# Adaptive-norm block with a long convolution and a Strassen FFN: the second layer norm moved from the convolution phase into the FFN's first pass

## Chip, cores, metric

One core of a Trainium2 chip. The metric is the device time of one execution in microseconds (us).

## What is computed

Input `u` is [4, 1024, 2048]: 4 batches of 1024 rows. A conditioning vector per batch gives six modulation vectors of 2048 (`sa, ca, ga` for the convolution, `sb, cb, gb` for the FFN). Cut to what matters:

```python
mod = (_silu(c) @ wmod).reshape(4, 6, 1, -1)
sa, ca, ga, sb, cb, gb = (mod[:, i] for i in range(6))
ga, gb = clip_magnitude(ga, 0.25), clip_magnitude(gb, 0.25)
h = _layernorm(x) * (1 + ca) + sa
x = x + ga * (causal_conv(h, K) + D * h)      # K: 2048 taps from the state-space parameters
h = _layernorm(x) * (1 + cb) + sb
x = x + gb * (h @ (W + low_rank).T + bias)    # 2048 x 2048
```

The convolution runs along the last axis, of 2048, so it is a multiplication of each row by a 2048 x 2048 Toeplitz matrix.

## The kernel before

The 4096 rows are 32 row tiles of 128 rows (`r`); two row tiles make one FFN unit (`u`, 16 of them). A phase for setup comes first, which computes the taps, builds the Toeplitz blocks and loads the first sections of `wmod`.

**Convolution phase, loop `r` in `net` (L925).** For each row tile:

- `conv_load` brings x (1 MB) into one of four x tiles. `stats` and `normalize` (L514, VectorE) give normalized rows in tile `n`. `conv_prep` transposes them in four groups of four 128x128 blocks (L535, TensorE against the identity, fp32, into a PSUM tile `tp`), modulates them out of PSUM with `ca`, `sa` per partition (L538, ScalarE) and splits them into fp16 high and low parts (L546, L547).
- `conv_mm` does the Toeplitz product (L567) in three families of fp16 matmuls; VectorE combines, gates and adds x (L584 to L594), which gives x1 in tile `y`, with row sums.
- `conv_post` stores x1 to DRAM (`x1d`), computes the second layer norm's mean and variance (L611, ScalarE's square with a running sum L614, `rstd`), normalizes (L617, VectorE, 128x2048, into a second `n` tile), then transposes the rows in four groups (L623, TensorE), copies each group out of PSUM (L624, ScalarE) and stores it to DRAM as `n2d` (L625, 256 KB per store).

The order is written by hand: `conv_mm` calls `tick()` ten times per row tile, and each call takes the letters of one entry of `PLAN`: S takes a step of the background work, P a step of the previous tile's `conv_post`, N one of the next tile's `conv_prep`, T the statistics and F the first step of the tile after. The background work is the merging of the low-rank update into the FFN weights (`merge`, eight parts) and the remaining modulation sections (`modps`, L317). From this order a scheduler with its own model of costs makes the final order of each engine's queue. Every engine then runs its queue in order. All large transfers are issued from SP's queue.

**FFN phase.** The FFN is a one-level Strassen product: per unit seven products of left factors (combinations of the four quarters of the transposed h, split in fp16 high and low) with seven merged weight combinations. A product is 24 matmuls of 128x512 (L704) into the PSUM tiles fX, fY, fZ. The loop has two passes `q` over the output columns. In pass 0, `left` (L645) makes the left factors of unit u+1, in program order after the matmuls of unit u: it loads `n2d` (L652, eight loads of 256 KB), modulates 16 blocks in SBUF with `cb`, `sb` (L654, ScalarE, 128x256), forms the combinations on VectorE (L671), casts them (L664, ScalarE) and takes the low part (L665, VectorE); `put` also stores each factor to `lfd` (512 KB). In pass 1, `left_again` loads the factors from `lfd`. `ffn_unit` (L693) loads the residual x1 (`xo`, two tiles of 512 KB per unit), adds the gated bias (L720), runs the products in the order 0, 4, 5, 1, 6, 2, 3, copies intermediate sums out of PSUM (L712, ScalarE: p1, p5, p6, p7), combines and gates them (`finish`, L725, L726), and stores the output once per row tile (L751, two stores of 512 KB). Unit 0's factors are made ahead, in the convolution phase.

```python
PLAN = ("PNS", "N", "NS", "NT", "PS", "PS", "PS", "PS", "FS", "SS")
...
            k.ffn_unit(pr, u, q, lf.pop(u), wc)
            if u + 1 < NU:
                lf[u + 1] = (k.left if q == 0 else k.left_again)(pr, u + 1)
```

PSUM has two tiles for transposes (`tps`), five for accumulation (`acc`) and one for modulation.

Of the kernel before, what the change touches and what calls it, by code (L numbers as in the profile page):

```python
# [24 lines left out]
P = 128  # L25
# [9 lines left out]
class Net:  # L35
# [254 lines left out]
    def prep_mod(self, pool):  # L290
# [8 lines left out]
        self.sct = self.const("sct", [P, 16, 8, NB])  # L299
# [24 lines left out]
    def mod_column(self, pool, name, plus_one):  # L324
# [7 lines left out]
        col = self.const(name, [P, NC, NB])  # L332
# [274 lines left out]
    def conv_post(self, pl, r, y, sums):  # L607
        nc, v = self.nc, self.nc.vector
        STQ(nc).dma_start(out=self.x1d[r], in_=y)
        mn = pl["sm"].tile([P, 1], F32, tag="mn", name="mn")  # L610
        v.tensor_scalar(mn, sums[:, 0:1], sums[:, 1:2], -1.0 / D, ADD, MUL)  # L611
        n = pl["n"].tile([P, D], F32, tag="n", name="n2")
        sq = pl["sm"].tile([P, 1], F32, tag="sq", name="sq")
        nc.scalar.activation(n, y, AF.Square, bias=mn, accum_out=sq)  # L614
        rs = pl["sm"].tile([P, 1], F32, tag="rs2", name="rs2")
        self.rstd(pl["sm"], sq, rs, 1, "r2", 1.0 / D)
        v.tensor_scalar(n, y, mn, rs, ADD, MUL)  # L617
        yield
        for c0 in range(0, NC, 4):
            nt = pl["nt"].tile([P, 4, P], F32, tag="nt", name="nt")  # L620
            tp = self.tps.tile([P, 4, P], F32, tag="t", name="tp2")
            for k in range(4):
                nc.tensor.transpose(tp[:, k], n[:, ds(P * (c0 + k), P)], self.ident)  # L623
            nc.scalar.copy(nt, tp)  # L624
            NTQ(nc).dma_start(out=self.n2d[r // 2][:, c0 : c0 + 4, r % 2, :], in_=nt)  # L625
            yield
# [18 lines left out]
    def left(self, pl, u):  # L645
        nc, v = self.nc, self.nc.vector
        b = u // 4
        t = pl["t"].tile([P, NC, 2, P], F32, tag="t", name="gt")
        for q in range(4):
            for h in range(2):  # L650
                sl = slice(HC * h + 2 * q, HC * h + 2 * q + 2)
                nc.sync.dma_start(out=t[:, sl], in_=self.n2d[u][:, sl])  # L652
                for c in range(sl.start, sl.stop):
                    nc.scalar.activation(  # L654
                        t[:, c], t[:, c], AF.Identity,
                        bias=self.sb[:, c, b : b + 1], scale=self.cb[:, c, b : b + 1],
                    )
        a11, a12 = t[:, 0:HC, 0, :], t[:, HC:NC, 0, :]
        a21, a22 = t[:, 0:HC, 1, :], t[:, HC:NC, 1, :]
        res = {}  # L660
# [8 lines left out]
        def comb(x, y, op, tag):  # L669
            t = pl["s"].tile([P, HC, P], F32, tag=tag, name=tag)  # L670
            v.tensor_tensor(t, x, y, op)  # L671
            return t

        put(0, a11)
        s1 = comb(a21, a22, ADD, "s1")
        put(4, s1)
        s2 = comb(s1, a11, SUB, "s2")
        put(5, s2)
        put(1, a12)
        put(6, comb(a11, a21, SUB, "s1"))  # L680
        put(2, comb(a12, s2, SUB, "s1"))
        put(3, a22)
        return res
# [9 lines left out]
    def ffn_unit(self, pl, u, q, lf, wc):  # L693
# [21 lines left out]
        xs = []  # L715
        for r in range(2):
            x = pl["o"].tile([P, 2, 512], F32, tag="o", name="xo")
            src = self.x1d[2 * u + r].rearrange("p (h n) -> p h n", h=2)[:, :, ds(512 * q, 512)]
            nc.sync.dma_start(out=x, in_=src)
            v.tensor_tensor(x, x, self.gbias, ADD)  # L720
            xs.append(x)

        def finish(r, h, cv):
            t = pl["e"].tile([P, 512], F32, tag="fin", name="fin")
            v.tensor_tensor(t, cv, self.gbt[:, h], MUL)  # L725
            v.tensor_tensor(xs[r][:, h], xs[r][:, h], t, ADD)  # L726
# [3 lines left out]
        p1 = copy("X", "p1")  # L730
        prod(4, "Y")
        p5 = copy("Y", "p5")
        prod(5, "Z")
        p6 = copy("Z", "p6")
        prod(1, "X")
        finish(0, 0, ps["X"])
        v.tensor_tensor(p6, p6, p1, ADD)
        prod(6, "Z")
# [3 lines left out]
        finish(1, 1, p7)  # L742
        prod(2, "Y")
        v.tensor_tensor(p6, p6, ps["Y"], ADD)
        finish(0, 1, p6)
        prod(3, "Z")
        v.tensor_tensor(p1, p1, ps["Z"], ADD)
        finish(1, 0, p1)
        for r in range(2):
            dst = self.io["out"][ds(256 * u + P * r, P), :].rearrange("p (h n) -> p h n", h=2)[:, :, ds(512 * q, 512)]  # L750
            STQ(nc).dma_start(out=dst, in_=xs[r])  # L751
# [7 lines left out]
PLAN = ("PNS", "N", "NS", "NT", "PS", "PS", "PS", "PS", "FS", "SS")  # L759
# [16 lines left out]
def net(ctx: ExitStack, tc: tile.TileContext, io):  # L776
# [5 lines left out]
    k.n2d = k.dram.tile([NU, P, NC, 2, P], F32, tag="n2d", name="n2d")  # L782
# [13 lines left out]
    def section(sec, pools):  # L796
# [5 lines left out]
        if sec == 0:  # L802
            k.sa = k.mod_column(msm, "sa", 0.0)
            k.hinv = k.fold_scale(msm, k.ca, k.sa, "fs1")
        elif sec == 1:
            k.ca = k.mod_column(msm, "ca", 1.0)
        elif sec == 2:
            k.gas, (k.gad,) = k.mod_gate(msm, "gad")
        elif sec == 4:
            k.cb = k.mod_column(msm, "cb", 1.0)  # L810
        elif sec == 3:
            k.sb = k.mod_column(msm, "sb", 0.0)
# [41 lines left out]
    for name, bufs in (("h", 2), ("n", 2), ("t", 2), ("y", 2), ("g", 1), ("nt", 2)):  # L854
# [33 lines left out]
    def early():  # L888
        right.close()
        for name, bufs in (("w", 1), ("l", 8), ("t", 1), ("s", 1)):  # L890
            pr[name] = pool(p2, "p2" + name, bufs, "right")
        load_w(0, ORDER[0])

# [27 lines left out]
    k.conv_late(xs.pop(0), *ys[0])  # L921
    take(k.conv_post(pl, 0, *ys[0]), 9)
    k.conv_late(xs.pop(1), *ys[1])
    post = k.conv_post(pl, 1, *ys[1])
    for r in range(2, 32):  # L925
# [6 lines left out]
        if r == LEFT0:  # L932
            while "w" not in pr:
                step()
            lf[0] = k.left(pr, 0)
# [3 lines left out]
        def tick():  # L939
            for a in next(plan):  # L940
                if a == "S":
                    step()
                elif a == "P":
# [95 lines left out]
```

## Time and profile before

| | |
|---|---|
| three runs | 2164.45 us median (2163.26 to 2166.11) |
| profiled execution | 2165.34 us, span 2163.6 us |
| granted TensorE clock, mean | 0.984 |
| TensorE busy | 2080.5 us, 11084 matmuls |
| VectorE busy | 1355.8 us |
| ScalarE busy | 938.8 us |
| DMA | 516.62 MB, mean 239 GB/s |
| last convolution matmul, first FFN matmul | 984.4 us, 984.5 us |
| start of the last FFN matmul | 2156.8 us |

In the profile PE is TensorE's matmuls, PEld its weight loads, DVE VectorE, ACT ScalarE, POOL GpSimd and SP the engine whose queue issues the DMAs. L704 is line 704 of the kernel. A group's row gives engine, operation, output and inputs, shape, count, then busy time and mean duration, then the engine's idle time in front of these instructions and what ended it. Matmuls overlap, so their busy times are longer than the distance between their starts.

### The profile page before, as it was taken

The numbers are of one execution on the slowest core, as the hardware profiler recorded it, in microseconds if no ns is written. First come the engines' busy times: TensorE is split into PE (matmuls) and PEld (weight loads), VectorE is DVE, ScalarE is ACT, GpSimd is POOL, SyncE is SP. The second block draws the span as 40 slices with busy tenths as digits, with TensorE's granted clock in tenths as the row PEclk, the third lists the DMA queues.
The fourth block names the chain that finished last, engine by engine and source line by source line (L and its number), as shares of the span: only waits on it lengthen the run. The fifth ranks groups of instructions, "written<-read, shape, count | busy, mean of one in ns | idle before, by whom it ended". The sixth has DMA issues, their size and how long they took to land.

```text
span 2163.6 us, 28506 instructions
## 1 busy us (share of the span) xinstructions
PE 2080.5 (96%) x11084; PEld 1019.0 (47%) x11084; DVE 1355.8 (63%) x2293; ACT 938.8 (43%) x1795; POOL 2.8 (0%) x12
## 2 busy tenths in 40 slices
PE   5698999999999999999999999999999999999998
PEld 1144555555555555564444444444444444444443
DVE  6538798889989999964665766666533333232333
ACT  1057677767776779862453535454200000000000
POOL 0000000000000000000000000000000000000000
PEclk8799999999999999999999999999999999999999
DMA  9988597888787657648756565656785544544541
GB/s 393 371 284 299 197 333 272 303 317 294 277 294 281 244 207 246 220 163 307 246 218 230 215 241 209 239 201 241 289 329 180 185 154 174 166 171 160 176 155 68
DMA packets 206497, 516.62 MB, mean 239 GB/s; under 512 B 15206, under 2 KB 80871, under 8 KB 179479
## 3 DMA queue, kind: packets, MB, share of 16 engines
q1 hardware_dynamic: 205824, 513.21, 66.3%
q8 instruction: 87, 1.43, 0.3%
q10 hardware_dynamic: 538, 1.59, 0.2%
q14 instruction: 48, 0.39, 0.1%
HBM read 325.89 MB, written 188.85 MB: 238 GB/s over the span
## 4 chain that ended last, share of the span: by engine, by line
PE 63%; DVE 15%; DMA 10%; ACT 9%; issue 2%; SPq 1%; POOL 0%; DVEq 0%; ACTq 0%
PE fZ L704 19%; PE fY L704 12%; PE fX L704 11%; PE ya L567 8%; PE yb L567 4%; PE modps L317 3%; DMA gt<-n2d 3%; PE lps L443 2%; ACT gt L654 2%; DVE lf L665 2%; PE tp L623 2%; ACT t L538 2%; ACT n L614 2%; DMA wm<-in_wmod 1%; DMA xo<-x1d 1%
## 5 line engine op out<-in xcount | busy, mean ns | idle before, releaser
L704 PEld LDWEIGHTS <-lf 128*128 128x128 f16 x5376 | 526.3, 98 | 643.0 <-issue 11.5
L704 PE MATMUL fZ<-w,lf 128*128 128x512 f16 x2304 | 514.8, 380 | 6.7 <-ACT p L712 6.7
L704 PE MATMUL fX<-w,lf 128*128 128x512 f16 x1536 | 342.6, 379 | 0.0
L704 PE MATMUL fY<-w,lf 128*128 128x512 f16 x1536 | 342.5, 379 | 0.0
L567 PEld LDWEIGHTS <-hc 128*128 128x128 f16 x2304 | 215.8, 98 | 190.7 <-issue 34.7
L720 DVE TENSOR_TENSOR xo<-xo,gb 128x1024 f32<-128x1024 f32 x64 | 78.4, 1224 | 207.0 <-DMA xo<-x1d 198.6
L538 ACT ACTIVATE t<-tp,sa,ca 128x128 f32<-128x128 f32 x512 | 199.6, 466 | 10.2 <-DVE sa L376 4.7
L654 ACT ACTIVATE gt<-gt,sb,cb 128x256 f32<-128x256 f32 x256 | 132.7, 592 | 151.7 <-DMA gt<-n2d 151.6
L567 PE MATMUL ya<-kh,hc 128*128 128x512 f16 (+3 forms) x768 | 192.6, 326 | 1.8 <-ACT qs L580 1.8
L567 PE MATMUL ya<-kh,hs 128*128 128x512 f16 (+3 forms) x768 | 193.3, 327 | 0.5 <-ACT hs L546 0.3
L567 PE MATMUL yb<-kh,hc 128*128 128x512 f16 (+3 forms) x768 | 193.0, 326 | 0.0
L317 PE MATMUL modps<-wm,sct 128*32 128x512 f32 x768 | 123.5, 687 | 32.2 <-DMA wm<-in_wmod 23.1
L567 PEld LDWEIGHTS <-hs 128*128 128x128 f16 x1152 | 107.6, 98 | 98.0 <-issue 17.7
L712 ACT COPY p<-fZ 128x512 f32<-128x512 f32 x64 | 37.3, 582 | 256.6 <-PE fZ L704 256.6
L712 ACT COPY p<-fX 128x512 f32<-128x512 f32 x32 | 18.5, 578 | 267.8 <-PE fX L704 254.9
L567 PE MATMUL ya<-kl,hs 128*128 128x512 f16 (+3 forms) x384 | 125.4, 326 | 0.0
L567 PE MATMUL yb<-kl,hc 128*128 128x512 f16 (+3 forms) x384 | 125.4, 326 | 0.0
L567 PE MATMUL ya<-kl,hc 128*128 128x512 f16 (+3 forms) x384 | 125.1, 326 | 0.0
L664 ACT CAST lf<-s 128x1024 f16<-128x1024 f32 x64 | 67.2, 1049 | 105.1 <-DVE s L671 78.7
L624 ACT COPY nt<-tp 128x512 f32<-128x512 f32 x128 | 74.9, 594 | 62.9 <-PE tp L623 43.3
L547 DVE TENSOR_TENSOR hc<-t,hc 128x512 f16<-128x512 f32 x128 | 87.5, 684 | 9.7 <-ACT hc L546 9.7
L535 PE MATMUL tp<-ident,n 128*128 128x128 f32 x512 | 79.4, 279 | 13.1 <-ACT t L538 11.6
(236 smaller groups left out, 2227.2 us busy)
## 6 DMA issues: line engine op xcount, KB each, us to landing
wm<-in_wmod SPq DMA_DIRECT2D x96, 1024.0 KB
lfd<-lf SPq DMA_DIRECT2D x112, 512.0 KB
lf<-lfd SPq DMA_DIRECT2D x112, 512.0 KB
x<-in_x SPq DMA_DIRECT2D x32, 1024.0 KB
x1d<-y SPq DMA_DIRECT2D x32, 1024.0 KB
n2d<-nt SPq DMA_DIRECT2D x128, 256.0 KB
gt<-n2d SPq DMA_DIRECT2D x128, 256.0 KB
xo<-x1d SPq DMA_DIRECT2D x64, 512.0 KB
```

Of the source, the lines that this page charges most:

```text
L317: self.last = self.nc.tensor.matmul(self.modps[32 * g : 32 * g + 32, :], self.sct[:, j].rearrange("p r b -> p (r b)"), w[:, ds(512 * g, 512)],
L443: nc.tensor.matmul(ps, la[:, x, k, h], y[:, k, osl], start=(n == 0), stop=(n == 5))
L535: nc.tensor.transpose(tp[:, k], n[:, ds(P * (c0 + k), P)], self.ident)
L538: nc.scalar.activation(t[:, k], tp[:, k], AF.Identity, bias=self.sa[:, c, b : b + 1], scale=self.ca[:, c, b : b + 1],)
L547: v.tensor_tensor(lo[:, sl], src, hi[:, sl], SUB)
L567: nc.tensor.matmul(pf[:, o:512], h, self.kf[f][z][:, ds(k0, 512 - o)], start=first, stop=(i == last and (x, z) == (1, 0)), skip_group_chec ...
L624: nc.scalar.copy(nt, tp)
L654: nc.scalar.activation(t[:, c], t[:, c], AF.Identity, bias=self.sb[:, c, b : b + 1], scale=self.cb[:, c, b : b + 1],)
L664: nc.scalar.copy(hl[:, :, 0, :], s)
L704: nc.tensor.matmul(ps[name], lf[i][:, k, x, :], wc[i][k // 4][:, k % 4, y, :], start=(first and n == 0), stop=(n == 3 * HC - 1), skip_grou ...
L712: nc.scalar.copy(t, ps[name])
L720: v.tensor_tensor(x, x, self.gbias, ADD)
```

## The change

`conv_post` no longer normalizes, transposes and stores `n2d`. It writes two numbers per row to a small tile `ln2`: 1/std and -mean/std. The square goes into the x tile, which has been read by then. `n` has one buffer instead of two, the `nt` and `n2d` tiles are gone.

`left` becomes a generator. Its first step loads two x1 row tiles from `x1d` (1 MB each) and normalizes each on ScalarE, in place (`x*scale + bias`, 128x2048). Eight steps follow, each with four fp32 transposes into one PSUM tile and two modulations out of PSUM (128x256) into `t`. A last step makes the seven factors, with one VectorE scratch tile and in-place operations instead of two scratch tiles. In the FFN's first pass `ffn_unit` calls `tick()` after each product, and `LPLAN` says what it takes: two transpose steps after each of the first four products, the factors after the fifth, load and normalization of the unit after next at the sixth. In the convolution phase the letter L in `PLAN` does the same for unit 0 in the last two row tiles.

`ffn_unit` also handles the residual and the output in four tiles of 256 KB per unit in place of two of 512 KB (five buffers), stores each as soon as it is done, and reuses p6, p7 and p1 for the gated values. `cb`, `sb` and the modulation inputs get their tiles from other pools.

```diff
-    def conv_post(self, pl, r, y, sums):
+    def conv_post(self, pl, r, x, y, sums):
         STQ(nc).dma_start(out=self.x1d[r], in_=y)
...
-        nc.scalar.activation(n, y, AF.Square, bias=mn, accum_out=sq)
-        rs = pl["sm"].tile([P, 1], F32, tag="rs2", name="rs2")
+        nc.scalar.activation(x, y, AF.Square, bias=mn, accum_out=sq)
+        rs = self.ln2[:, r, 1:2]
         self.rstd(pl["sm"], sq, rs, 1, "r2", 1.0 / D)
-        v.tensor_scalar(n, y, mn, rs, ADD, MUL)
-        yield
-        for c0 in range(0, NC, 4):
-            nt = pl["nt"].tile([P, 4, P], F32, tag="nt", name="nt")
-            tp = self.tps.tile([P, 4, P], F32, tag="t", name="tp2")
-            for k in range(4):
-                nc.tensor.transpose(tp[:, k], n[:, ds(P * (c0 + k), P)], self.ident)
-            nc.scalar.copy(nt, tp)
-            NTQ(nc).dma_start(out=self.n2d[r // 2][:, c0 : c0 + 4, r % 2, :], in_=nt)
-            yield
+        v.tensor_tensor(self.ln2[:, r, 0:1], mn, rs, MUL)

-    def left(self, pl, u):
+    def left(self, pl, u, res):
+        xs = []
+        for r in range(2):
+            x = pl["x2"].tile([P, D], F32, tag=f"x2{r}", name="x2")
+            nc.sync.dma_start(out=x, in_=self.x1d[2 * u + r])
+            nc.scalar.activation(
+                x, x, AF.Identity, bias=self.ln2[:, 2 * u + r, 0:1], scale=self.ln2[:, 2 * u + r, 1:2]
+            )
+            xs.append(x)
+        yield
         t = pl["t"].tile([P, NC, 2, P], F32, tag="t", name="gt")
-        for q in range(4):
-            for h in range(2):
-                sl = slice(HC * h + 2 * q, HC * h + 2 * q + 2)
-                nc.sync.dma_start(out=t[:, sl], in_=self.n2d[u][:, sl])
-                for c in range(sl.start, sl.stop):
-                    nc.scalar.activation(t[:, c], t[:, c], AF.Identity, ...)
+        for c0 in range(0, NC, 2):
+            tp = self.tps.tile([P, 2, 2, P], F32, tag="t", name="tp2")
+            for c in range(2):
+                for r in range(2):
+                    nc.tensor.transpose(tp[:, c, r], xs[r][:, ds(P * (c0 + c), P)], self.ident)
+            for c in range(2):
+                nc.scalar.activation(
+                    t[:, c0 + c], tp[:, c], AF.Identity,
+                    bias=self.sb[:, c0 + c, b : b + 1], scale=self.cb[:, c0 + c, b : b + 1],
+                )
+            yield
...
         put(0, a11)
-        s1 = comb(a21, a22, ADD, "s1")
-        put(4, s1)
-        s2 = comb(s1, a11, SUB, "s2")
-        put(5, s2)
+        s = pl["s"].tile([P, HC, P], F32, tag="s", name="s")
+        v.tensor_tensor(s, a21, a22, ADD)
+        put(4, s)
+        v.tensor_tensor(s, s, a11, SUB)
+        put(5, s)
         put(1, a12)
-        put(6, comb(a11, a21, SUB, "s1"))
-        put(2, comb(a12, s2, SUB, "s1"))
+        v.tensor_tensor(a21, a11, a21, SUB)
+        put(6, a21)
+        v.tensor_tensor(s, a12, s, SUB)
+        put(2, s)
         put(3, a22)

     def ffn_unit(...):
-        for r in range(2):
-            x = pl["o"].tile([P, 2, 512], F32, tag="o", name="xo")
+        for r, h in ((0, 0), (1, 1), (0, 1), (1, 0)):
+            x = pl["o"].tile([P, 512], F32, tag="o", name="xo")
...
         prod(0, "X")
         p1 = copy("X", "p1")
+        tick()
         prod(4, "Y")
         p5 = copy("Y", "p5")
+        tick()
         prod(5, "Z")
         p6 = copy("Z", "p6")
+        tick()
         prod(1, "X")
...
+        tick()
         prod(6, "Z")
         p7 = copy("Z", "p7")
...
+        tick()
         prod(2, "Y")
...
+        tick()
         prod(3, "Z")
...
-PLAN = ("PNS", "N", "NS", "NT", "PS", "PS", "PS", "PS", "FS", "SS")
+PLAN = ("PNSL", "NL", "NSL", "NTL", "SL", "SL", "SL", "SL", "FSL", "SSL")
+LPLAN = ("LL", "LL", "LL", "LL", "L", "0", "")

     # net, FFN loop
-            k.ffn_unit(pr, u, q, lf.pop(u), wc)
-            if u + 1 < NU:
-                lf[u + 1] = (k.left if q == 0 else k.left_again)(pr, u + 1)
+            def tick():
+                if q == 1:
+                    return
+                for a in next(plan):
+                    if a == "0":
+                        gens[0] = next_left(u + 2)
+                    take(gens[0], 1)
+            k.ffn_unit(pr, u, q, lf.pop(u), wc, tick)
+            if q == 1 and u + 1 < NU:
+                lf[u + 1] = k.left_again(pr, u + 1)
```

## Prediction

> **What bounds the kernel now.** I read the page first, for the shares and the slices; then the groups by line, for the steps that the change touches; then a table of stretches; then the timeline of TensorE, to get what one instruction really costs there.
>
> The page, busy shares and the chain that ended last:
>
> ```profile
> PE 2080.5 (96%) x11084; PEld 1019.0 (47%) x11084; DVE 1355.8 (63%) x2293; ACT 938.8 (43%) x1795; POOL 2.8 (0%) x12
> ...
> DVE  6538798889989999964665766666533333232333
> ...
> PE 63%; DVE 15%; DMA 10%; ACT 9%; issue 2%; SPq 1%; POOL 0%; DVEq 0%; ACTq 0%
> ```
>
> TensorE is busy nearly everywhere, and VectorE comes close to it in the first 18 slices (the convolution phase, to about 985 us). So two questions decide: how much TensorE work moves, and what TensorE waits for in each phase.
>
> A busy matmul is not its price, because matmuls overlap. The timeline of TensorE inside the convolution phase (start, busy time, instruction):
>
> ```profile
> 505.94 0.22 PE L567 MATMUL ya<-kh,hs 128*128 128x128 f16 x1
> 506.00 0.60 PE L535 MATMUL tp<-ident,n 128*128 128x128 f32 x4
> 506.44 0.38 PE L567 MATMUL yb<-kh,hc 128*128 128x512 f16 x1
> 506.65 0.38 PE L567 MATMUL yb<-kl,hc 128*128 128x512 f16 x1
> ```
>
> Four fp32 transposes are issued in 0.44 us (506.00 to 506.44), 0.109 each, though the page calls one 0.277 busy. A 128x512 fp16 matmul takes 0.216, so one product of 24 takes 5.18, and a matmul follows a transpose group without a gap.
>
> Stretches of 108 us: sum, PE, PEld, DVE, ACT and POOL busy with instruction counts, granted clock, DMA share, GB/s. The first two end the convolution phase, the next four are the FFN's first pass, the last is its second pass:
>
> ```profile
> 648.00:756.00 108.00, 106.58 (x673) 59.98 (x672) 99.32 (x194) 80.56 (x165) 0.00 (x0) 1.00 0.75 267
> 756.00:864.00 108.00, 103.03 (x665) 62.58 (x664) 103.81 (x216) 90.41 (x191) 0.38 (x1) 1.00 0.64 222
> 1080.00:1188.00 108.00, 102.94 (x468) 46.06 (x467) 68.94 (x77) 49.28 (x78) 0.00 (x0) 0.98 0.62 224
> 1188.00:1296.00 108.00, 106.63 (x494) 48.22 (x493) 70.26 (x79) 52.30 (x83) 0.00 (x0) 1.00 0.63 227
> 1296.00:1404.00 108.00, 107.93 (x500) 48.85 (x499) 70.52 (x78) 52.38 (x83) 0.00 (x0) 1.00 0.61 224
> 1404.00:1512.00 108.00, 107.77 (x500) 48.69 (x498) 71.17 (x79) 49.49 (x78) 0.00 (x0) 1.00 0.62 221
> 1728.00:1836.00 108.00, 108.00 (x502) 48.99 (x501) 34.79 (x46) 6.45 (x11) 0.00 (x0) 1.00 0.48 167
> ```
>
> The second pass is full: 502 matmuls per stretch. Against that the first pass lacks 34, 8, 2 and 2 matmuls, 46 x 0.216 = 9.9 us. That is all the first pass can still gain. VectorE at 103.8 of 108 shows where the convolution phase might have a second limit.
>
> Groups by line (busy, mean ns | idle before it, and what ended it):
>
> ```profile
> L654 ACT ACTIVATE gt<-gt,sb,cb 128x256 f32<-128x256 f32 x256 | 132.7, 592 | 151.7 <-DMA gt<-n2d 151.6
> L535 PE MATMUL tp<-ident,n 128*128 128x128 f32 x512 | 79.4, 279 | 13.1 <-ACT t L538 11.6 <-ACT nt L624 0.7 <-DVE mn L611 0.4
> L623 PE MATMUL tp<-ident,n 128*128 128x128 f32 x512 | 77.9, 277 | 9.5 <-ACT t L538 4.9 <-DVE n L617 2.5 <-ACT nt L624 2.0
> L624 ACT COPY nt<-tp 128x512 f32<-128x512 f32 x128 | 74.9, 594 | 62.9 <-PE tp L623 43.3 <-DMA n2d<-nt 16.1 <-issue 1.1
> L614 ACT ACTIVATE n<-y,mn 128x2048 f32<-128x2048 f32 x32 | 64.1, 2002 | 23.0 <-DVE mn L611 22.8
> L617 DVE TENSOR_SCALAR n<-y,mn,rs 128x2048 f32<-128x2048 f32 x32 | 43.0, 1343 | 0.5
> ```
>
> **The change, part by part.**
>
> *Transposes move (TensorE).* 512 leave the convolution phase. In the built order of the changed kernel, unit 0's 32 are still done there, between the convolution matmuls of the last two row tiles; the other 480 stand in the first pass, eight after each of a unit's first four products. At 0.109 that is 52.3 us off one phase and 52.3 onto the other: zero, as long as both are TensorE's.
>
> A rule speaks against zero. The Trainium skill, TensorE: Matmul & The Clock Gate, Part 4, gives a transpose about 275 ns in a kernel's context and says that transposes do not count as busy for the clock gate. If the moved ones cost that in the first pass and gave back only 109, the sum would be an estimated 480 x 0.166 = 80 us worse. The rows above (0.44 for four, granted clock 1.00 in a phase with such groups throughout) say otherwise, and I take them.
>
> *Waits in front of those transposes go.* The L623 row shows 9.5 us idle. Taken start to start over the timeline, less the pitches above, it is 17 us, since the overlap hides some 0.17 of each wait. Some of it will turn up before the next instruction. Bounds 0 and 17; I take 12.
>
> *ScalarE and VectorE get lighter in the convolution phase.* 128 evictions of 594 ns (75 us) and 32 normalizations of 1343 ns (43 us) go; 32 one-column multiplies of about 0.2 us come. Neither engine sets that phase alone, so most of this buys nothing, but L535's waits for ScalarE (11.6) should ease. Bounds 0 and 7 (its share after startup); I take 2. The square is the same 2.0 us and now writes the x tile, which a load needs a whole row tile later; one n buffer instead of two is enough, as the transposes of a tile end in step 4 of 10 and the next normalization is in step 9.
>
> *DMAs.* 128 stores and 128 loads of 256 KB through n2d go, 32 loads of 1 MB from x1d come. SP's queue gets shorter; in a pass-1 unit 2 MB are read either way.
>
> *The first pass, one unit.* Let 0 be the end of the fourth set of transposes. TensorE then has the last three products (to 5.2, 10.4, 15.5) and the next unit's first (20.7), after which it needs both rows normalized. SP issues the first row's load at 0, as soon as the old x2 is read; the second about 1.2 later, behind one output store. ScalarE is in order: normalization of row one (2.0 us, by L614's row of the same shape), copy p7 (0.58), three casts (1.05 each), normalization of row two, two casts. Behind the first normalization stands p7, which the third of those products needs at 10.4. So the load may land as late as 10.36 - 0.58 - 2.0 = 7.8. For 1 MB the rows give 2.7 us (392 GB/s in the first 54 us) to 8.5 (the longest wait for n2d's 2 MB in the chain); I take 5, nearer to the first, since few DMAs are queued then. Row one done at 7, p7 at 7.6, row two at about 13: no wait. Each pair of transpose groups finds its two PSUM banks emptied: copy 0.58 plus four modulations of 0.47 to 0.59 end 3 us after a product, and the next pair comes 5.18 after. ScalarE's unit: 16 x 0.55 + 7 x 1.05 + 2 x 2.0 + 3 x 0.58 = 22 of 40 us; VectorE's stays as it is.
>
> So 9.9 us of waits (they come from modulations held until n2d lands, 151.6 us on ScalarE) largely go. The start stays rough: unit 0's residual tiles load behind 9 weight loads, the built order puts unit 1's x2 loads behind an output store, and its eight groups then run in a burst in which six wait for an eviction, 6 x (2 x 0.55 - 0.44) = 4 us, plus 0 to 5 for the late load; I take 2. Waits 6 in place of 9.9: gain 4, bounds -10 and 9.9 (the low end: 1 us more in ten units).
>
> *Tail.* The last store is 256 KB and not 512 KB: gain 0 to 1, I take 0.5.
>
> Sum: 12 + 2 + 4 + 0.5 = 18.5. The profiled execution took 2165.34 us (span 2163.6), so 2146.8; the median of the runs lies 0.9 below it. I say 2147.
>
> **Rivals.**
>
> *Load too late, slower.* Pass 1 gains a wait if the first x2 row lands after 7.8: each unit then loses the excess, since ScalarE holds p7 and TensorE its third product. At 10 us that is 15 x 2.2 = 33, so 2147 + 33 = 2180. For it: the chain has waits of 7 to 8.5 us for n2d in this pass. Against: those are 2 MB in eight issues. It beats the gain from 7.8 + 18.5 / 15 = 9.0 on. Chance 0.15.
>
> *VectorE keeps the convolution phase long.* In the two stretches from 648 to 864 it is busy 203.1 us for about 8.5 row tiles; less 8.5 x 1.34 it is 191.7. TensorE's account wants these 216 us to shrink by 8.5 x 1.75 + 8 = 23, to 193. If VectorE cannot pass the 94% it has now, they shrink only to 204, and 11 us are lost: 2158. Against: unit 0's combines, some 13 us, also leave this stretch. Chance 0.17.
>
> *Groups cost their busy time.* If each of 120 groups takes 0.60 and not 0.44 between products, 19 us come back: 2166, no change. Against: the matmul at 506.44. Chance 0.08.
>
> *As summed:* 0.60; its own range is 2137 to 2155 (all waits gone, or half).
>
> **How the numbers follow.** About 0.2%, 4 us, is what a measurement of this kernel can tell from no change. Faster: 0.60, 0.14 of the VectorE case and a little of the late load (0.01 to 9.0 us): 0.75. Same: 0.07 of the third and 0.01 of the second: 0.08. Slower: 0.14 of the late load, 0.02 of the VectorE case and 0.01 of the third: 0.17. The range runs from 2136 to 2170, leaving out most of the late-load case.
>
> **What would show it.** Right: about 502 TensorE starts plus the transposes in each stretch of the first pass from its third unit on; the new transposes 0.44 a group with the granted clock at 1.00; the convolution phase ending near 916 (985 - 52 - 14, and a little), the first pass 47 to 50 us longer. Wrong: ScalarE idle for x2<-x1d with TensorE's third product behind p7 (the late load), idle before L535 or the convolution matmuls ended by VectorE (the second rival), or the convolution phase ending after 935.

## The result and the profile after

The changed kernel takes 2149.73 us (median of 4 runs, 2145.42 to 2151.66), the kernel before 2165.05 in the same comparison (4 runs, 2163.26 to 2166.11). The ratio is 0.9927, with a 95% interval of 0.9909 to 0.9945: faster, by some 16 us. The profiled execution took 2148.25 us, with a span of 2146.5 (before: 2165.34 and 2163.6). The prediction was 2147 us, range 2136 to 2170.

The page of the changed kernel: busy shares, VectorE's slices, and the chain that ended last.

```profile
PE 2077.2 (97%) x11084; PEld 1021.9 (48%) x11084; DVE 1322.7 (62%) x2357; ACT 926.2 (43%) x1699; POOL 3.4 (0%) x12
...
DVE  6549789988999998666565566565433323332323
...
PE 75%; DVE 11%; ACT 5%; DMA 2%; issue 1%; SPq 0%; POOL 0%; ACTq 0%; DVEq 0%
```

TensorE has the same 11084 matmuls. Its share of the chain rose from 63% to 75%, and what it took came from DMA (10% to 2%), VectorE (15% to 11%) and ScalarE (9% to 5%). VectorE's run of eights and nines ends one slice of 54 us earlier.

The timeline of TensorE in the first pass of the changed kernel (start, busy time, instruction):

```profile
1136.69 1.67 PE L703 MATMUL fY<-w,lf 128*128 128x512 f16 x7
...
1138.20 1.04 PE L653 MATMUL tp<-ident,x 128*128 128x128 f32 x8
...
1139.07 5.13 PE L703 MATMUL fZ<-w,lf 128*128 128x512 f16 x23
```

Eight transposes from 1138.20 to 1139.07: 0.87 us, 0.109 each, between two products, with no wait on either side. Every pair of groups from the third unit of the pass on (after 1012 us) looks like this one.

The same stretches as before (sum, PE, PEld, DVE, ACT and POOL busy with counts, granted clock, DMA share, GB/s):

```profile
648.00:756.00 108.00, 103.41 (x624) 57.49 (x622) 102.00 (x211) 82.16 (x168) 0.38 (x1) 0.98 0.51 185
756.00:864.00 108.00, 105.45 (x663) 61.42 (x661) 97.15 (x230) 71.35 (x167) 0.00 (x0) 1.00 0.39 147
1080.00:1188.00 108.00, 108.00 (x546) 54.57 (x544) 65.26 (x79) 56.17 (x80) 0.00 (x0) 1.00 0.55 200
1188.00:1296.00 108.00, 108.00 (x542) 54.06 (x540) 67.89 (x80) 55.26 (x75) 0.00 (x0) 1.00 0.61 219
1296.00:1404.00 108.00, 108.00 (x546) 54.55 (x545) 63.70 (x74) 58.52 (x82) 0.00 (x0) 1.00 0.55 201
1404.00:1512.00 108.00, 108.00 (x550) 55.05 (x549) 62.13 (x77) 53.66 (x81) 0.00 (x0) 1.00 0.53 187
1728.00:1836.00 108.00, 108.00 (x502) 48.98 (x501) 33.90 (x51) 7.03 (x12) 0.00 (x0) 1.00 0.51 165
```

The first pass is now as full as the second: 108.00 busy of 108.00, clock 1.00. The counts are higher than 502 because a transpose takes half a matmul's time. The convolution phase (first two rows) is not full: TensorE lacks 4.6 and 2.6 us there, while VectorE is busy 102.0 and 97.2 of 108. The clock of 0.98 in the first row is a stretch of 3.4 us at half speed (690.5 to 693.9) behind a stall of TensorE; the last section comes back to such stretches.

Groups by line, those that answer to the four groups around the transposes before:

```profile
L655 ACT ACTIVATE gt<-tp,sb,cb 128x256 f32<-128x256 f32 x256 | 124.9, 575 | 60.9 <-PE tp L653 60.9
L643 ACT ACTIVATE x<-x,ln 128x2048 f32<-128x2048 f32 x32 | 67.1, 2096 | 29.0 <-DMA x<-x1d 29.0
L535 PE MATMUL tp<-ident,n 128*128 128x128 f32 x512 | 80.6, 282 | 15.1 <-ACT t L538 11.8 <-DVE n L514 2.7
L653 PE MATMUL tp<-ident,x 128*128 128x128 f32 x512 | 68.2, 274 | 1.9 <-ACT x L643 1.5 <-ACT t L538 0.3
```

ScalarE's modulations no longer wait for a load (151.6 us before) but for TensorE (60.9), which costs nothing. Its new normalizations do wait 29.0 us for x1d, yet TensorE waits only 1.5 us for them. In front of L535, TensorE still waits; that did not ease.

By the trace, the time went as follows ("convolution end" is the start of the last convolution matmul, "FFN" runs from there to the start of the last FFN matmul):

| us | before | after | difference |
|---|---|---|---|
| convolution end | 984.4 | 924.8 | -59.6 |
| FFN | 1172.4 | 1215.9 | +43.5 |
| tail behind the last matmul | 6.7 | 5.8 | -0.9 |

Before, 16 of the 512 transposes already lay in the FFN; after, 480. So 464 x 0.109 = 50.6 us changed sides. What the change gained beyond that is 59.6 - 50.6 = 9.0 in the convolution phase, 50.6 - 43.5 = 7.1 in the FFN, and 0.9 in the tail: 17 us of the profiled executions. Of the 9.0, 1.1 us is setup, whose length varies anyway: the first convolution matmul starts at 111.5 us before and 110.4 after, and between 108.9 and 112.8 over all traces of this study.

### The profile page after: what moved, and what is told of

The parts are those of the page before. It is cut to its first block, busy times and chain, and to the rows that moved or that the text cites. A ratio compares the mean times of both kernels' runs of the same rounds, so it can differ in the third digit from the quotient of the medians.

```text
span 2146.5 us, 28399 instructions
## 1 busy us (share of the span) xinstructions
PE 2077.2 (97%) x11084; PEld 1021.9 (48%) x11084; DVE 1322.7 (62%) x2357; ACT 926.2 (43%) x1699; POOL 3.4 (0%) x12
## 4 chain that ended last, share of the span: by engine, by line
PE 75%; DVE 11%; ACT 5%; DMA 2%; issue 1%; SPq 0%; POOL 0%; ACTq 0%; DVEq 0%
PE fZ L703 22%; PE fX L703 15%; PE fY L703 15%; PE ya L567 10%; PE yb L567 5%; PE tp L653 3%; PE lps L443 2%; PE modps L317 2%; ACT x L613 1%; PE tp L535 1%; ACT t L538 1%; DVE y L594 1%; DVE st L497 1%; DVE hc L547 1%; DVE wch L471 1%
## 5 line engine op out<-in xcount | busy, mean ns | idle before, releaser
L721 DVE TENSOR_TENSOR xo<-xo,gb 128x512 f32<-128x512 f32 x128 | 87.8, 690 | 242.0 <-DMA xo<-x1d 229.6
L538 ACT ACTIVATE t<-tp,sa,ca 128x128 f32<-128x128 f32 x512 | 201.3, 473 | 13.2 <-DVE sa L376 5.1
L655 ACT ACTIVATE gt<-tp,sb,cb 128x256 f32<-128x256 f32 x256 | 124.9, 575 | 60.9 <-PE tp L653 60.9
L726 DVE TENSOR_TENSOR fin<-fX,gb 128x512 f32<-128x512 f32 x32 | 22.1, 692 | 128.0 <-PE fX L703 127.9
L535 PE MATMUL tp<-ident,n 128*128 128x128 f32 x512 | 80.6, 282 | 15.1 <-ACT t L538 11.8
L443 PE MATMUL lps<-lbh,lac 128*128 128x512 f16 x256 | 85.6, 382 | 1.3 <-ACT lbh L418 0.8
```

Of the source, the lines that this page charges most:

```text
L443: nc.tensor.matmul(ps, la[:, x, k, h], y[:, k, osl], start=(n == 0), stop=(n == 5))
L538: nc.scalar.activation(t[:, k], tp[:, k], AF.Identity, bias=self.sa[:, c, b : b + 1], scale=self.ca[:, c, b : b + 1],)
L655: nc.scalar.activation(t[:, c0 + c], tp[:, c], AF.Identity, bias=self.sb[:, c0 + c, b : b + 1], scale=self.cb[:, c0 + c, b : b + 1],)
L721: v.tensor_tensor(x, x, self.gbias[:, h], ADD)
```

## The experiments

The theory at the start: TensorE sets both phases, a transpose is worth 0.109 us in either, so the moved work cancels and the gain is waits that went with the groups. The rivals: a transpose costs more; a load comes too late; VectorE holds the convolution phase. All ratios below are to the kernel before, run side by side (its median there was 2168 to 2170 us, so a ratio says more than a median); 0.9927 is the changed kernel. The two columns on the right are of one profiled execution each. Kernels that share their convolution phase end it at 924.8, 924.6, 926.2 and 927.5 us (the changed kernel, dvenorm, burst, dload) and at 984.4 and 985.9 (the kernel before, quarters), so a difference of up to 3 us there says nothing.

| kernel | median, us | ratio (95%) | convolution end | FFN |
|---|---|---|---|---|
| conv_double | 2219.06 | 1.0230 (1.0213 to 1.0247) | 1035.0 | 1176.1 |
| ffn_double | 2206.70 | 1.0172 (1.0157 to 1.0188) | 932.4 | 1267.5 |
| burst | 2163.31 | 0.9973 (0.9963 to 0.9984) | 926.2 | 1228.3 |
| dload | 2169.91 | 1.0008 (0.9996 to 1.0021) | 927.5 | 1234.0 |
| quarters | 2195.03 | 1.0116 (1.0097 to 1.0134) | 985.9 | 1202.8 |
| traffic | 2150.36 | 0.9908 (0.9891 to 0.9926) | 927.3 | 1215.0 |
| dvespare | 2163.68 | 0.9974 (0.9961 to 0.9987) | 940.1 | 1215.2 |
| actspare | 2163.88 | 0.9977 (0.9968 to 0.9986) | 942.3 | 1215.4 |
| actnorm | 2144.66 | 0.9887 (0.9868 to 0.9906) | 918.0 | 1215.7 |
| nonorm | 2158.01 | 0.9952 (0.9936 to 0.9968) | 978.1 | 1170.7 |
| n2act | 2181.80 | 1.0058 (1.0044 to 1.0073) | 998.5 | 1174.8 |
| dvenorm | 2152.57 | 0.9924 (0.9908 to 0.9939) | 924.6 | 1216.2 |

### What a transpose costs: conv_double and ffn_double

On the kernel before:

```diff
-            for k in range(4):
+            for k in (0, 1, 2, 3, 0, 1, 2, 3):
                 nc.tensor.transpose(tp[:, k], n[:, ds(P * (c0 + k), P)], self.ident)
```

> The kernel before, with every group of four transposes of the second norm issued twice in the convolution phase: 512 more fp32 transposes there, nothing else. Theory of the prediction (TensorE sets the time of this phase, a transpose is worth its 0.109 us): 512 x 0.109 = 56 us more, less what fits into the 17 us that TensorE waits in front of these groups anyway: 2165 + 39 to 56 = 2204 to 2221 us. Rival (VectorE holds the phase, so that moving TensorE's work out of it wins little): the added work lies beside VectorE's, 2165 to 2185 us.

On the changed kernel:

```diff
-            for c in range(2):
+            for c in (0, 1, 0, 1):
                 for r in range(2):
                     nc.tensor.transpose(tp[:, c, r], xs[r][:, ds(P * (c0 + c), P)], self.ident)
```

> The changed kernel with each of the new groups of four transposes issued twice: 512 more transposes, 480 of them in the first pass of the FFN, nothing else. Theory (TensorE sets the time, the clock stays at 1.00): 512 x 0.109 = 56 us more, 2206 us; the waits between groups can only shrink, so 2200 to 2208. Rival (a transpose costs its busy time of 0.274 us, or it lets the clock fall): 512 x 0.274 = 140 us, 2290 us, or a granted clock under 0.97 in the first pass. Rival (the groups lie beside other work): under 2175 us.

The convolution end came 50.6 us later for 512 transposes more, of which 496 lie there (54.1 at 0.109): nearly all of their time, although VectorE is nearly full. The FFN became 51.6 longer for 480 more (52.3 at 0.109). The first pass with twice the transposes, in two of the stretches:

```profile
1080.00:1188.00 108.00, 108.00 (x582) 58.80 (x580) 57.77 (x68) 51.15 (x72) 0.00 (x0) 1.00 0.52 183
1188.00:1296.00 108.00, 108.00 (x581) 58.86 (x580) 62.15 (x76) 53.03 (x74) 0.00 (x0) 1.00 0.56 197
```

Still no gap, still clock 1.00. The price is close to 0.109 us on both sides (0.102 and 0.108 by these differences), and the move itself is worth next to nothing. The rival of the busy time is out.

### Where the groups stand: burst

```diff
-LPLAN = ("LL", "LL", "LL", "LL", "L", "0", "")
+LPLAN = ("", "", "", "", "LLLLLLLLL", "0", "")
```

> The changed kernel with all eight groups of a unit asked for at once, behind the fifth product of the unit before, in place of two behind each of the first four. As ordered on TensorE, two groups then run at once and each further group behind two more matmuls of the sixth product. Theory (two PSUM banks, ScalarE empties a group in 2 x 0.575 = 1.15 us, the groups come every 4 x 0.109 + 2 x 0.217 = 0.87 us): six groups of a unit wait 0.28 us each, 1.7 us a unit, times the 14 units that are prepared so: 24 us, 2174 us, with 2160 to 2195 as bounds, since ScalarE also has the copies of the products in this stretch. Rival (where the groups stand does not matter, VectorE and ScalarE have room enough): 2150 within 4 us.

Inside the bounds, but with the wrong sizes: 12.4 us more in the FFN in place of 24. The timeline of one such burst:

```profile
1034.30 7.41 ACT L655 ACTIVATE gt<-tp,sb,cb 128x256 f32<-128x256 f32 x16
...
1035.37 0.66 PE L653 MATMUL tp<-ident,x 128*128 128x128 f32 x4
...
1035.87 0.59 PE L703 MATMUL fY<-w,lf 128*128 128x512 f16 x2
...
1036.30 0.64 PE L653 MATMUL tp<-ident,x 128*128 128x128 f32 x4
```

ScalarE's 16 modulations take 7.41 us, 0.463 each, though the page gives one a mean of 0.597: back to back they overlap, as TensorE's matmuls do. So ScalarE empties a group in 0.93 us, not 1.15, and the groups run every 0.91 us against 0.87 without a wait. By the distances between TensorE's starts a unit lost some 0.5 us in its eight groups, 7 to 8 us over the pass; another 7 us came from one stall at the change of passes (4.9 us waiting for ScalarE's copy of fZ, and 2 us of slow matmuls behind it, see the last section). Two groups behind each product is the better place, and it is worth less than I thought.

### A later load: dload

```diff
             nc.sync.dma_start(out=x, in_=self.x1d[2 * u + r])
+            nc.sync.dma_start(out=x, in_=self.x1d[2 * u + r])
             nc.scalar.activation(
```

> The changed kernel with each load of an x1 row tile for the second norm issued twice into the same tile, so that a row tile is complete about 10 us after its issue in place of 5.3 and 32 MB more are read. In the order of this kernel both normalizations stand behind the copy p7 and the second row's transposes 5 to 6 us later. Theory (the lateness of a load costs nothing until its row is normalized later than its first transposes; 10 + 2.1 and 20 + 2.1 us after the fourth set of transposes, against slots at 21 and 27): 2150 within 6 us. Rival of the prediction (a late load stalls TensorE: allowed 7.8 us, landed after 10, 2 to 3 us for each of 14 units): 2180 us or more.

It fell between the two: 18 us in the FFN. A row of the timeline of ScalarE and TensorE, in a unit in the middle of the pass:

```profile
1352.60 2.10 ACT L644 ACTIVATE x<-x,ln 128x2048 f32<-128x2048 f32 x1 [3.65 <-DMA x<-x1d]
...
1354.75 0.64 PEld L654 LDWEIGHTS tp<-ident,x 128*128 128x128 f32 x6 [0.44 <-ACT x L644]
```

The second row is normalized just as its transposes are due (0.44 us late here, up to 2.7 in other units; TensorE waited 9.6 us for such rows in all). My threshold of 7.8 us is not tested by this run, because the scheduler put the copy p7 ahead of both normalizations here.

The changed kernel's own trace comes close to testing it. From the third unit on, p7's copy usually ends 2.2 to 2.5 us before TensorE's third product needs fZ, and the second row is normalized 5.6 to 8.0 us before its transposes. In one unit the first load was late, and its normalization started 7.7 us after the fourth set of transposes:

```profile
1278.14 2.09 ACT L643 ACTIVATE x<-x,ln 128x2048 f32<-128x2048 f32 x1 [3.67 <-DMA x<-x1d]
1280.14 0.56 ACT L711 COPY p<-fZ 128x512 f32<-128x512 f32 x1
...
1280.80 3.40 PE L703 MATMUL fZ<-w,lf 128*128 128x512 f16 x15
```

p7 was copied at 1280.70, and the product started at 1280.80 without a wait. So 7.7 us cost nothing, with 0.1 us to spare, as the prediction's 7.8 has it. In most other units a load could have come some 2.3 us later.

### The small pieces alone: quarters

On the kernel before, only the four quarter tiles of residual and output:

```diff
-            x = pl["o"].tile([P, 2, 512], F32, tag="o", name="xo")
+        for r, h in ((0, 0), (1, 1), (0, 1), (1, 0)):
+            x = pl["o"].tile([P, 512], F32, tag="o", name="xo")
...
+            STQ(nc).dma_start(out=at(self.io["out"][ds(256 * u, 256), :], r, h), in_=x)
...
-        pr[name] = pool(p2l, "p2" + name, 3 if name == "o" else 1)
+        pr[name] = pool(p2l, "p2" + name, 5 if name == "o" else 1)
```

> The kernel before with only one part of the change: the residual xo is loaded, finished and stored in four quarter tiles of 128x512 in place of two halves, on five buffers in place of three; the second norm stays in the convolution phase. Theory: it takes about 1 us of the tail and touches the copies that TensorE waits for in the first pass (9.9 us) little: 2162 to 2165 us on the scale of 2165. Rival (the pieces, not the moved norm, gave the FFN's waits): 2156 to 2159 us.

Neither: 25 us slower by the ratio, 31 in the profiled executions. The tail did shrink by 0.9, but TensorE now waits for the copies out of PSUM. Its groups (6.7 us of waits before):

```profile
L704 PE MATMUL fZ<-w,lf 128*128 128x512 f16 x2304 | 523.5, 385 | 28.0 <-ACT p L712 28.0
```

Why copies of 0.56 us are late is seen in ScalarE's timeline. First the kernel before, around its longest stall (2.4 us, from 1155.7):

```profile
1149.87 1.09 ACT L654 ACTIVATE gt<-gt,sb,cb 128x256 f32<-128x256 f32 x2 [8.74 <-DMA gt<-n2d]
1151.77 0.60 ACT L654 ACTIVATE gt<-gt,sb,cb 128x256 f32<-128x256 f32 x1 [0.81 <-DMA gt<-n2d]
1152.28 0.56 ACT L712 COPY p<-fY 128x512 f32<-128x512 f32 x1
1152.74 5.02 ACT L654 ACTIVATE gt<-gt,sb,cb 128x256 f32<-128x256 f32 x10
1157.67 0.56 ACT L712 COPY p<-fZ 128x512 f32<-128x512 f32 x1
```

ScalarE stood idle for 8.74 us for a load of n2d, then ran ten modulations in one go, and the copy of fZ had its place behind them. TensorE could not write fZ again before 1158. With quarter tiles the same happens and the load is later still (between the last two rows stand a copy, the last modulation and three casts, two of which wait for VectorE):

```profile
1537.60 1.09 ACT L654 ACTIVATE gt<-gt,sb,cb 128x256 f32<-128x256 f32 x2 [13.26 <-DMA gt<-n2d]
...
1543.67 4.53 ACT L654 ACTIVATE gt<-gt,sb,cb 128x256 f32<-128x256 f32 x9 [1.75 <-DMA gt<-n2d]
...
1553.78 0.58 ACT L712 COPY p<-fZ 128x512 f32<-128x512 f32 x1
```

SP's queue has twice as many residual loads and output stores between the n2d loads, and many of them wait for VectorE. In the changed kernel the same quarter tiles cost nothing that shows: its modulations come out of PSUM behind TensorE's own transposes, and two loads a unit stand in ScalarE's order in place of eight. So, by these waits, the FFN's 7 us come from the loads taken out of that order; against the kernel before with quarter tiles they are 38 us (waits of 41.1 and 3.5, start to start). That the queue's order makes the n2d loads late is read from the waits, and was not tried by itself.

### What the convolution phase gained from: traffic, dvespare, actspare

Three things left the phase beside the transposes: 33.6 MB of stores, 43 us of VectorE, 75 us of ScalarE. Each is put back by itself, in `conv_post` of the changed kernel, with nobody reading what it writes:

```diff
 # traffic
+        for c0 in range(0, D, 512):
+            NTQ(nc).dma_start(out=self.n2d[r, :, c0 : c0 + 512], in_=y[:, c0 : c0 + 512])
 # dvespare
+        v.tensor_scalar(x, y, mn, rs, ADD, MUL)
 # actspare
+        for c0 in range(0, D, 512):
+            nc.scalar.copy(x[:, c0 : c0 + 512], y[:, c0 : c0 + 512])
```

> The changed kernel with the stores that the change took out of the convolution phase put back as dummies: 1 MB for each row tile in four pieces, 33.6 MB in all, from the row tile y as soon as it is complete. Theory (queues and DMA engines are not on the path of the convolution phase): 2150 to 2153 us. Rival (the 9 us that the phase gained beyond the transposes come from the lighter DMA traffic): the phase ends some 9 us later, 2158 to 2162 us.

> The changed kernel with VectorE's normalization pass of the second norm (128x2048, about 1.3 us) put back for each row tile in the convolution phase, its result unused: 32 x 1.34 = 43 us more of VectorE there. Rival of the prediction (VectorE keeps the convolution phase long, so its relief made the gain): the phase ends 9 us later or more, 2159 us and up. Theory (the waits went with the groups that stood in front of them): 2150 to 2154 us.

> The changed kernel with ScalarE's copies of the second norm's transposes put back as dummies in the convolution phase: four copies of 128x512 for each row tile, from the finished row tile into a tile that nobody reads, 128 x 0.59 = 75 us more of ScalarE there. If ScalarE's relief carries part of the gain (on the kernel before, 67 us more for ScalarE undid the 10 us of a relieved VectorE and cost 12 besides, some 23 in all): the phase ends 5 to 20 us later, 2155 to 2170 us. If only VectorE's relief counts: 2150 to 2153 us.

The traffic counts for nothing that can be measured (the end moved by 2.5 us, the time not at all). VectorE's pass moved the end by 15.3 us, ScalarE's copies by 17.5. Each alone takes back the whole gain of the phase and more. These are prices of the work where it stands here: actspare has the four copies of a row tile (71 us in all, as measured) in one piece, which the kernel before had spread over four steps. That x is held longer by them is not the reason, since VectorE waited only 0.7 and 1.6 us for loads of x in these runs. A part of the time is seen in front of the first norm's transposes: start to start, TensorE waits there 5.3 us more in dvespare and 7.6 more in actspare than in the changed kernel; the rest is spread over the matmuls of the convolution, the merging and the modulation. The group of dvespare, then that of actspare (15.1 us of waits in the changed kernel):

```profile
L535 PE MATMUL tp<-ident,n 128*128 128x128 f32 x512 | 79.8, 281 | 19.2 <-ACT t L538 14.4 <-DVE n L514 4.6
```

```profile
L535 PE MATMUL tp<-ident,n 128*128 128x128 f32 x512 | 80.1, 281 | 21.4 <-ACT t L538 19.4 <-DVE n L514 1.8
```

Against the changed kernel (11.8 and 2.7), the waits for ScalarE's modulation L538 and VectorE's normalization L514 both grew in the first, and the one for L538 alone in the second.

### The same on the other side: nonorm, n2act, actnorm, dvenorm

`nonorm` is the kernel before without VectorE's second normalization pass (the transposes take `y`), `n2act` the kernel before with the pass on ScalarE:

```diff
 # nonorm
-        v.tensor_scalar(n, y, mn, rs, ADD, MUL)
...
-                nc.tensor.transpose(tp[:, k], n[:, ds(P * (c0 + k), P)], self.ident)
+                nc.tensor.transpose(tp[:, k], y[:, ds(P * (c0 + k), P)], self.ident)
 # n2act
-        v.tensor_scalar(n, y, mn, rs, ADD, MUL)
+        v.tensor_tensor(mr, mn, rs, MUL)
+        nc.scalar.activation(n, y, AF.Identity, bias=mr, scale=rs)
```

> The kernel before with VectorE's normalization pass of the second norm left out (the transposes take the row tile y as it is; mean and deviation are still computed): the second norm's values are not normalized. All transposes, copies and stores stay in the convolution phase; VectorE loses 32 x 1.34 = 43 us. With the pass put back into the changed kernel the phase ended 15 us later. If what that showed is VectorE's load alone, the waits of TensorE shrink here too: 2149 to 2158 us on the scale of 2165. If the waits belong to the groups of transposes that stand here (my first reading), 2162 to 2166 us.

> The kernel before with that pass computed on ScalarE (2.1 us for a row tile, 67 us in all; ScalarE is busy 0.75 of the phase) in place of VectorE, all else as it was. If VectorE's load is what counts: 2152 to 2161 us, since the first norm's pass, moved in the same way in the changed kernel, gave 5 us. If ScalarE's time weighs as much: 2163 us and up, and the copies of the transposes wait behind it.

VectorE's relief, with all transposes in their place, ends the phase 6.3 us earlier and the whole 8 us in the profiled executions, some 10 by the ratio. That is what VectorE's load was expected to give (0.9952 of 2165 is 2155), and against my first reading. It is not the load alone, though: start to start, 3.8 us of it is in front of the second norm's own transposes, which in this run need no result of the pass at all. But given to ScalarE the pass costs 14 us in the phase: ScalarE's 67 us weigh more than VectorE's 43 there. The second norm's transposes wait no longer for it than before (15.9 us start to start, against 15.4), those of the first norm 9.6 us longer (the part of their row that ScalarE's L538 ended grew from 11.6 to 16.3); so what costs is ScalarE's time, not a longer pass in front of its own transposes.

`actnorm` is the changed kernel with the first norm's pass on ScalarE, `dvenorm` the changed kernel with the new pass in the FFN on VectorE:

```diff
 # actnorm
-ACTNORM = ""
+ACTNORM = "1"
 # dvenorm
-            nc.scalar.activation(
-                x, x, AF.Identity, bias=self.ln2[:, 2 * u + r, 0:1], scale=self.ln2[:, 2 * u + r, 1:2]
-            )
+            v.tensor_scalar(x, x, self.ln2[:, 2 * u + r, 1:2], self.ln2[:, 2 * u + r, 0:1], MUL, ADD)
```

> The changed kernel with the first norm's normalization moved from VectorE to ScalarE throughout the convolution phase: VectorE is relieved of about 43 us there, ScalarE gets 67 us (2.1 us for a row tile). If VectorE still holds parts of the phase (busy 102 of 108 us at 648 to 756 us), the phase ends 5 to 10 us earlier, 2140 to 2145 us. If TensorE's own work sets it, 2150 within 3 us; if ScalarE's longer pass in front of the transposes counts, up to 2165 us.

> The changed kernel with the new normalization in the FFN on VectorE (1.34 us) in place of ScalarE (2.1 us for a row tile). Theory (neither engine is late in the first pass of the FFN, where TensorE waits about 3 us in all): 2150 within 3 us. Rival (ScalarE's long pass in front of the copies is what the waits of the first units come from): 2146 us or less.

The changed kernel has ScalarE room in the convolution phase, and here the exchange pays: the phase ends at 918.0, 6.8 us earlier, and the profiled span is 2139.5 against 2146.5. The group of the first norm's transposes in actnorm:

```profile
L535 PE MATMUL tp<-ident,n 128*128 128x128 f32 x512 | 79.3, 280 | 11.4 <-ACT t L538 7.0 <-ACT n L512 3.7
```

Waits of 11.4 us in place of 15.1. By its median this is the fastest kernel of the study; it was not timed side by side with the changed kernel, but the intervals of the two ratios, 0.9868 to 0.9906 and 0.9909 to 0.9945, do not meet. In the FFN the engine of the pass makes no difference (dvenorm: 0.9924), as expected: both have room there.

## Why the prediction was right, and where it was not

**Transposes move, net 0.** Right, with both sides of it measured: close to 0.109 us each, clock 1.00. (464 changed sides, not 480: 16 stood in the FFN before.) The rule weighed against it (the Trainium skill, TensorE: Matmul & The Clock Gate, Part 4), by which the sum would have been an estimated 80 us worse, does not hold for these fp32 groups between dense matmuls: the first pass ran 480 and then 960 of them at a granted clock of 1.00. The page's 275 ns is near the busy time here (274), but that is not the pitch. Nor did the clock treat transposes as idle time. In ffn_double's second unit 3.4 us hold 29 transposes and one matmul, and the clock stays at 1.00 behind them, where 2.04 us without any work were enough for half speed elsewhere (last section):

```profile
996.20:999.60 3.40, 3.40 (x30) 2.91 (x29) 0.62 (x2) 3.10 (x6) 0.00 (x0) 1.00 0.03 5
999.60:1003.00 3.40, 3.40 (x18) 1.61 (x17) 1.23 (x1) 1.98 (x5) 0.00 (x0) 1.00 0.35 142
```

**Waits in front of those transposes, 12, and relief of ScalarE and VectorE, 2.** Together 14 predicted, 9.0 measured, and the split is wrong. I had the waits belong to the groups that stand there, and had the relief buy nearly nothing, because neither engine sets the phase alone. The waits of L623 did go, 15.4 us of them in this phase start to start, but some 7 came back in front of other instructions, most of it in front of the convolution's matmuls into ya (4.9) and L535 (2.5). So that term was nearer 8 than 12, and even this needed the relief: with VectorE's pass put back the phase gains nothing beyond the transposes (it ends at 940.1; 984.4 - 50.6 would be 933.8), and the same with ScalarE's copies (942.3). L535's waits did not ease as I had said (13.1 to 15.1). With 50 us less of TensorE's work the two other engines have less time for a row tile, and what left them was about made up by that: VectorE's share did not fall at all; 216 to 864 us, before:

```profile
216.00:864.00 648.00, 633.08 (x3987) 351.42 (x3988) 578.32 (x1132) 484.04 (x981) 0.38 (x1) 0.99 0.77 272
```

and after:

```profile
216.00:864.00 648.00, 635.88 (x3919) 339.27 (x3918) 581.54 (x1220) 446.35 (x935) 0.38 (x1) 0.99 0.64 237
```

578 and 582 us busy. The step that failed is "Neither engine sets that phase alone, so most of this buys nothing": it prices the relief in the old balance, and the move changes the balance. In the new one, either relief taken away cost more than the whole gain. What stays open is the exact share of each engine, since their effects do not add: 15.3 and 17.5 us, each of which alone is more than the 9.0 there were.

**The rival of VectorE.** The phase ended at 924.8, not after 935, and the time was not 2158: as a forecast it did not come true. As a mechanism it was the nearest to what went on. Its working compared VectorE's own 191.7 us with TensorE's 193 and so saw that the two would be even; dvespare, with 43 us more of VectorE, lands at 0.9974, near that rival's 2158.

**First pass.** Predicted waits 6 in place of 9.9; measured 3.5 in place of 10.6 (start to start). The mechanism is as written (modulations held until n2d lands), steady state has none, and the rest is in the first two units. The gain of 4 became 7 because the burst of the second unit cost 0.7 us and not 4: the term `6 x (2 x 0.55 - 0.44)` took ScalarE's mean durations as its pace, and the burst run measured 0.463 a modulation. The late load there took 1.7 us (2 predicted).

**The x2 loads.** From issue to landing they took a median of 5.3 us where I took 5:

```profile
x<-x1d SPq DMA_DIRECT2D x32, 1024.0 KB, 5.3
```

From the third unit on no third product had to wait for p7, so the late load's rival fell by the trace. How near it was is shown by the unit with 0.1 us to spare, and by dload, in another order: loading each row twice cost 18 us in the FFN. The 8.5 us that I gave as the longest wait for n2d in the chain is the longest in the first pass; the one for unit 0, in the convolution phase, was 9.4.

**Tail.** 0.5 predicted, 0.9 measured. The quarter tiles that give it were costed at nothing else, which is right in the changed kernel and wrong by 30 us in the old one.

**Sum.** 14 became 9.0, 4 became 7.1, 0.5 became 0.9: 18.5 against 17.0. The total is right partly because a term too large and one too small made up for each other: in this there was luck. The 916 that I gave for the end of the convolution phase does not follow from its own terms, which make 919; it ended at 924.8, since 9.0 and not 14 came on top of the transposes, and those were 50.6 and not 52.

## What to carry to other kernels

When work is moved off a stage whose other engines are nearly as full as the bound, count what leaves those engines too: they get less time per item, and without their relief part of the move comes back as waits. A moved instruction on a dense engine is worth its distance from start to start, on both sides; busy time and mean duration, on ScalarE too, are no pace. And look at what an in-order engine has between two short copies that the bound waits for: a load awaited there delays the copies behind it, and the bound with them (8.7 us of waiting on ScalarE became a stall of 2.4 us on TensorE), and cutting other transfers into pieces may push that load back further.

## What was not expected of the hardware

A stall of TensorE can cost more than itself. Behind the 2.4 us stall of the kernel before, the granted clock is at half for 3.41 us. In each of the fourteen traces all changes of the clock lie on one grid of steps of 3.413 us. The kernel before in steps of its grid, with the stall in the first (idle is the length less PE's busy time):

```profile
1155.89:1159.31 3.42, 1.18 (x6) 0.48 (x5) 1.20 (x2) 3.42 (x8) 0.00 (x0) 1.00 0.11 41
1159.31:1162.72 3.41, 3.41 (x9) 1.22 (x8) 3.41 (x5) 2.39 (x3) 0.00 (x0) 0.50 0.00 0
1162.72:1166.13 3.41, 3.41 (x17) 1.57 (x16) 3.41 (x5) 2.56 (x3) 0.00 (x0) 1.00 0.46 181
```

And quarters, first a stall of 3.4 us that fell across two steps, then the one of 5.4 us:

```profile
1392.49:1395.91 3.42, 1.42 (x7) 0.55 (x6) 3.42 (x4) 1.74 (x3) 0.00 (x0) 1.00 0.22 87
1395.91:1399.32 3.41, 2.22 (x11) 1.03 (x11) 3.41 (x4) 2.09 (x3) 0.00 (x0) 1.00 0.73 287
...
1549.52:1552.93 3.41, 0.00 (x0) 0.00 (x0) 3.41 (x4) 1.73 (x3) 0.00 (x0) 1.00 0.14 54
1552.93:1559.76 6.83, 5.35 (x13) 1.87 (x13) 6.79 (x8) 3.42 (x4) 0.00 (x0) 0.50 0.70 280
```

The matmuls at half speed start 0.43 us apart in place of 0.216, seven to fourteen of them, which adds 1.4 to 2.9 us to each such stall. Over the FFN of all fourteen traces, none of the stalls between 1.2 and 2.1 us was followed by it, 9 of the 12 between 2.4 and 3.6 us were, and both longer ones (4.9 and 5.4). What goes with it is the idle time inside one step. From 240 to 2130 us half speed begins 22 times in these traces: 21 times TensorE had been idle for 2.04 us or more of the step before, once for 1.76 (ffn_double, convolution phase). No other step at full speed had more than 2.01 us. So in these runs a stall split by the grid, like the one of 3.4 us above, went free; why 1.76 was once enough stays open.

The Trainium skill (TensorE: Matmul & The Clock Gate, Part 1) tells of a window of about 3.4 us that runs freely, and of half speed after one idle window. The grid agrees with such a window, but about 2 us of idle time in it were enough here, less than the page's idle window. In quarters such slow matmuls cost some 10 us in the FFN, against 2 in the kernel before, so some 8 of the 30 us that its FFN lost.
